# Layer 0's attention product as 64x64 blocks in the four quarters of the array, with a copy of h whose graphs are exchanged

## The chip, the core and the metric

The kernel runs on one core of a Trainium2 chip. Everything is in fp32. The metric is the device time of one execution in microseconds, lower being better. The kernel before takes 3661.84 us, the median of three runs that lie between 3660.82 and 3661.86.

A core has a matrix engine (TensorE, PE in the profile), whose weight loads are shown apart (PEld), and VectorE (DVE), ScalarE (ACT), GpSimd (POOL) and SyncE (SP), which here issues all DMAs. Matmul results land in PSUM, all other data is in SBUF. Both memories have 128 partitions.

## What is computed

The input x holds 128 graphs of 64 nodes with 768 features. Two attention layers follow each other, each with a residual and a layernorm. The change concerns layer 0, cut here to what matters:

```python
h = jnp.einsum('bnd,ade->bane', feat_in, W)              # 12 heads of 64
th = jnp.tanh(h)
attn_src = jnp.einsum('bane,aeo->bano', th, w_src)
attn_dst = jnp.einsum('bane,aeo->bano', th, w_dst)
attn = attn_src + jnp.swapaxes(attn_dst, 2, 3)
attn = jnp.where(attn >= 0, attn, LEAKY_ALPHA * attn)
attn = jnp.where(mask, jnp.float32(-999.0), attn)
attn = jax.nn.softmax(attn, axis=-1)                     # 64 x 64 for each graph and head
feat_out = jnp.einsum('banm,bame->bane', attn, h) + b
feat_out = jax.nn.elu(feat_out)
gate = jax.nn.sigmoid(feat_in @ H_w.T + H_b)
x = layernorm(x + gate * feat_out + (1.0 - gate) * feat_in)
```

The fourth line from the end, the probabilities of a graph times h, is the aggregation that is changed. For one graph and one head it is a product of two 64x64 matrices. Layer 1 is ordinary attention with 6 heads of 128 over the same graphs.

## The kernel before

**Tiles, units, groups.** A tile is 128 tokens on the partitions, that is two graphs of 64 nodes; there are 64 tiles. A unit of layer 0 is half the heads (6 of 12, 384 columns) of one tile, so there are 128 units. A group is two tiles, thus four units. Layer 1 works by groups.

**One unit of layer 0** runs through four functions, two of them a unit later:

- `l0_products(u)` makes h in PSUM (six matmuls of 384 columns at L177), copies it to SBUF on VectorE (L246), takes its tanh, forms the source and destination terms of the attention on GpSimd and VectorE, and makes the gate's product.
- `l0_probs(u)` spreads the destination term by one matmul (L280) and runs the mask and the softmax over `s`, 128 partitions (graph, query) by 6 heads by 64 keys.
- `l0_probs_transposed(u - 1)` turns `s`: three 128x128 transposes, two heads in each (L202). A transposed block has head parity and key on its partitions and graph and query on its columns. Four copies of 64x192 (L209) then put the blocks into `pts[0]`, which is 128x128 for each head and block-diagonal over the two graphs; its other blocks were zeroed once at the start.
- `l0_rest(u - 1)` multiplies: six matmuls of a 128x128 block-diagonal stationary with 64 columns of h (L303), into one PSUM tile `po`. Then VectorE adds the bias (L308), and the elu, the gate, the residual and, after a tile's second half, the layernorm follow.

**Order of the work.** The loop at the end emits, for each unit u, the products of u, the transposes of u-1, some pieces of layer 1, the probabilities of u, the rest of u-1, and more pieces of layer 1. `quota` spreads a group's pieces of layer 1 evenly over four units. A framework then sets the order on each engine when the program is built, by the priority of the code's order and by which instructions it takes to be ready; it also chooses VectorE or ScalarE for every `nc.any.tensor_copy`. Within an engine's queue, SP's among them, that order is fixed. All waits are on semaphores which the framework adds.

**Buffers.** `xp` holds 7 tiles of x; a tile stays from its load to the store of the result, and six pieces of H_w pass through the same buffers at the start. `work` has 2 buffers for most tiles and 3 for h. PSUM is split into 4 banks for products (`psm`) and 4 for everything else (`psa`): transposes, L280, the aggregation's `po`, layer 1's scores (L355) and context (L379).

Layer 1's scores at L355 write 64 columns of the array at a time: one graph to PSUM partitions 0 to 63, the other to 64 to 127. Layer 1 has its own block-diagonal tile, `pts[1]`, filled by `probs_transposed`.

Of the kernel before, what the change touches and what calls it, by code (L numbers as in the profile page):

```python
# [9 lines left out]
F32 = mybir.dt.float32  # L10
# [5 lines left out]
P = 128  # L16
# [7 lines left out]
def kernel(  # L24
# [17 lines left out]
    bf: bass.AP,  # L42
    out: bass.AP,
):
    """Two graph-attention layers, each followed by a residual and a layernorm.

    A tile is 128 tokens on the partitions: two graphs of 64 nodes. A group is G tiles, whose
    q and k share a pass over the weights. All products are in fp32.
    """
    nc = tc.nc  # L50
    NB, S, D = x.shape
    A, _, E = W.shape
# [13 lines left out]
    adj_g = adj.rearrange("(q t g) n m -> q (g n) t m", t=G, g=2)  # L66

    const = ctx.enter_context(tc.tile_pool(name="const", bufs=1))
    xp = ctx.enter_context(tc.tile_pool(name="xp", bufs=7))
    big = ctx.enter_context(tc.tile_pool(name="big", bufs=1))  # L70
    work = ctx.enter_context(tc.tile_pool(name="work", bufs=2))
    small = ctx.enter_context(tc.tile_pool(name="small", bufs=3))
    psm = ctx.enter_context(tc.tile_pool(name="psm", bufs=4, space=bass.MemoryType.PSUM))
    psa = ctx.enter_context(tc.tile_pool(name="psa", bufs=4, space=bass.MemoryType.PSUM))

# [1 line left out]
    ident = const.tile([P, P], F32, name="ident")  # L77
    make_identity(nc, ident)
    eye = const.tile([P, S], F32, name="eye")
# [19 lines left out]
        load_x(t)  # L99
    load_adj(0)  # L100

# [1 line left out]
    def rows(src, name):  # L103
        n = src.shape[0]
        t = const.tile([P, n], F32, name=name)
# [45 lines left out]
    bv_c = columns(bv, "bv_c")  # L151
    bf_bc = rows(bf, "bf_bc")

    # Transposed probabilities of AH heads, block-diagonal over the tile's two graphs: only the
    # diagonal blocks are written after this. One for each layer.
    pts = [const.tile([P, AH, P], F32, name=f"pt{i}") for i in range(2)]
    for pt in pts:
        nc.gpsimd.memset(pt, 0.0)

# [1 line left out]
    def halves(h):  # L161
        return slice(h * HALF, (h + 1) * HALF)

    def transposed(src, dst):
        """dst[:, c, :] = src[:, chunk c].T"""
        for half in range(2):
            ps = psa.tile([P, CH, P], F32, name="pa")
            for c in range(CH):
                k = half * CH + c
                nc.tensor.transpose(ps[:, c, :], src[:, k * P : (k + 1) * P], ident)  # L170
            nc.any.tensor_copy(dst[:, half * CH : (half + 1) * CH, :], ps)  # L171

    def product(lhsT, w, half):
        """One half of the columns of lhsT.T @ w in PSUM."""
        ps = psm.tile([P, HALF], F32, name="pm")
        for c in range(NC):
            nc.tensor.matmul(  # L177
                ps, lhsT[:, c, :], w[:, c, halves(half)], start=(c == 0), stop=(c == NC - 1)
            )
        return ps  # L180

    def softmax(s, n):
        """Over the last of s [P, n, S], in place."""
        mx = small.tile([P, AH], F32, name="mx")
        nc.vector.tensor_reduce(mx[:, :n], s, AX.X, ALU.max)  # L185
        nc.vector.tensor_tensor(
            s, s, mx[:, :n, None].to_broadcast([P, n, S]), ALU.subtract
        )
        nc.scalar.activation(s, s, AF.Exp)
        sm = small.tile([P, AH], F32, name="sm")  # L190
        nc.vector.tensor_reduce(sm[:, :n], s, AX.X, ALU.add)
        rs = small.tile([P, AH], F32, name="rs")
        nc.vector.reciprocal(rs[:, :n], sm[:, :n])  # L193
        nc.gpsimd.tensor_tensor(  # L194
            s, s, rs[:, :n, None].to_broadcast([P, n, S]), ALU.mult
        )

    def probs_transposed(s, pt):
        """s [P, AH, S] over (graph, query) -> [(graph, key), head, (graph, query)]."""
        ps = psa.tile([P, AH // 2, P], F32, name="pa")  # L200
        for j in range(AH // 2):
            nc.tensor.transpose(  # L202
                ps[:, j, :], s[:, 2 * j : 2 * j + 2, :].rearrange("p h m -> p (h m)"), ident
            )
        pt_v = pt.rearrange("p (j h) n -> p j h n", h=2)
        for g in range(2):
            own = slice(g * S, (g + 1) * S)
            for h2 in range(2):
                nc.any.tensor_copy(pt_v[own, :, h2, own], ps[h2 * S : (h2 + 1) * S, :, own])  # L209
# [20 lines left out]
        nc.vector.tensor_scalar(f1, a, 1.0, -L1_NEG, op0=ALU.subtract, op1=ALU.mult)  # L230
        masks[g] = (a, f0, f1)

# [1 line left out]
    xTs, units = {}, {}  # L234

    def l0_products(u):
        t, half = divmod(u, 2)
        hs = halves(half)
        if half == 0:
            xTs[t] = work.tile([P, NC, P], F32, name="xT")  # L240
            transposed(xs[t], xTs[t])
        xT = xTs[t] if half == 0 else xTs.pop(t)

        ph = product(xT, w_sb, half)
        h = work.tile([P, HALF], F32, name="h", bufs=3)
        nc.vector.tensor_copy(h, ph)  # L246
        th = work.tile([P, HALF], F32, name="th")
        nc.scalar.activation(th, ph, AF.Tanh)  # L248
        tmp = work.tile([P, HALF], F32, name="tmp", bufs=3)
        nc.gpsimd.tensor_tensor(tmp, th, ws_bc[:, hs], ALU.mult)  # L250
        sd = small.tile([P, 2, AH], F32, name="sd")
        nc.vector.tensor_reduce(
            sd[:, 0, :], tmp.rearrange("p (a e) -> p a e", a=AH), AX.X, ALU.add
        )
        nc.gpsimd.tensor_tensor(th, th, wd_bc[:, hs], ALU.mult)
        nc.vector.tensor_reduce(
            sd[:, 1, :], th.rearrange("p (a e) -> p a e", a=AH), AX.X, ALU.add
        )
        # dst on the diagonal: what same_graph spreads along the free axis
        dg = work.tile([P, AH, S], F32, name="tmp", bufs=3)  # L260
        nc.gpsimd.tensor_tensor(
            dg,
            eye[:, None, :].to_broadcast([P, AH, S]),
            sd[:, 1, :, None].to_broadcast([P, AH, S]),
            ALU.mult,
        )

        # gate = (1 + tanh(y / 2)) / 2
        pg = product(xT, hw_sb, half)
        gt = work.tile([P, HALF], F32, name="gt")  # L270
        nc.vector.tensor_tensor(gt, pg, hb_bc[:, hs], ALU.add)
        nc.scalar.activation(gt, gt, AF.Tanh, scale=0.5)
        units[u] = [h, gt, sd, dg]

    def l0_probs(u):
        g, i = divmod(u // 2, G)
# [14 lines left out]
        units[u][2:] = [s]  # L291

    def l0_probs_transposed(u):
        probs_transposed(units[u].pop(), pts[0])

    def l0_rest(u):
        t, half = divmod(u, 2)
        hs = halves(half)
        xt = xs[t]
        h, gt = units.pop(u)  # L300
        po = psa.tile([P, AH, E], F32, name="pa")
        for a in range(AH):
            nc.tensor.matmul(  # L303
                po[:, a, :], pts[0][:, a, :], h[:, a * E : (a + 1) * E], start=True, stop=True
            )
        # elu(z) + 1 = max(z, 0) + exp(min(z, 0))
        z = work.tile([P, HALF], F32, name="z")
        nc.vector.tensor_tensor(  # L308
            z.rearrange("p (a e) -> p a e", a=AH),
            po,  # L310
            b_bc[:, None, :].to_broadcast([P, AH, E]),
            ALU.add,
        )
        e = work.tile([P, HALF], F32, name="tmp", bufs=3)
        nc.vector.tensor_scalar_min(e, z, 0.0)  # L315
        nc.scalar.activation(e, e, AF.Exp)  # L316
        nc.vector.scalar_tensor_tensor(z, z, 0.0, e, op0=ALU.max, op1=ALU.add)
        nc.vector.scalar_tensor_tensor(
            z, z, 1.0, xt[:, hs], op0=ALU.subtract, op1=ALU.subtract
        )  # L320
        # the residual's sum, doubled, as the layernorm's epsilon then is fourfold:
        # 2 * (2 * x + gate * (elu - x)) = 4 * x + (1 + tanh(y / 2)) * (elu - x)
        nc.vector.scalar_tensor_tensor(z, gt, 1.0, z, op0=ALU.add, op1=ALU.mult)  # L323
        nc.vector.scalar_tensor_tensor(  # L324
            xt[:, hs], xt[:, hs], 4.0, z, op0=ALU.mult, op1=ALU.add
        )
        if half == 1:
            layernorm(xt, 4.0 * EPS)

# [1 line left out]
    def layer1(g):  # L331
        x1T = big.tile([P, NC, G, P], F32, name="x1T")
        for i in range(G):
# [39 lines left out]
        def context(i):  # L373
            cTs[i] = work.tile([P, HEADS, P], F32, name="cT", bufs=1)
            for half in range(2):
                pc = psa.tile([P, CH, P], F32, name="pa")
                for j in range(CH):
                    hd = half * CH + j
                    nc.tensor.matmul(  # L379
                        pc[:, j, :],  # L380
                        vs[i][:, hd * P : (hd + 1) * P],
                        pts[1][:, hd, :],
                        start=True,
                        stop=True,
                    )
                # a row's probabilities sum to one, so v's bias goes straight to the context
                hds = slice(half * CH, (half + 1) * CH)
                nc.vector.tensor_tensor(  # L388
                    cTs[i][:, hds, :], pc, bv_c[:, hds, None].to_broadcast([P, CH, P]), ALU.add
# [13 lines left out]
        pieces += [(0, probs, (i,)) for i in range(G)]  # L403
        pieces += [(4, values, (0, 0)), (4, values, (0, 1))]
        for i in range(G):
            pieces.append((1, lambda i: probs_transposed(s[:, i], pts[1]), (i,)))
            if i + 1 < G:
                pieces.append((4, values, (i + 1, 0)))
            else:
# [5 lines left out]
        pieces += [(4, result, (G - 1, 0)), (4, result, (G - 1, 1))]  # L415
        return pieces

# [1 line left out]
    assert G == 2  # L419
    UG = 2 * G  # L420
    LAG = 2
# [62 lines left out]
```

## Time and profile before

| | us |
|---|---|
| median of the runs | 3661.84 |
| span of the profiled execution, first to last instruction | 3657.3 |
| TensorE busy | 3605.6 |
| VectorE busy | 1721.5 |
| ScalarE busy | 810.4 |
| GpSimd busy | 852.3 |

The profile is of one execution, and its span lies 4.5 us under the median of the runs. Times in the profile count from its first instruction. L303 is line 303 of the kernel. In a line on a group of instructions stand the line, the engine, the operation, what is written and read, the size and the count; then busy time and the mean duration of one in ns; then the engine's idle time just before them and what ended it. In a line of a timeline stand the start and the time covered by all instructions of that line. Matmuls are pipelined, so their durations overlap: what one costs is the distance from its start to the next. A matmul in fp32 shows as two instructions, each with its own load of weights.

A group of four units takes 112.6 us in the steady part; the first units, without layer 1 beside them, are slower than their matmuls as one chain of small steps has nothing to fill its waits.

### The profile page before, as it was taken

The numbers are of one execution on the slowest core, as the hardware profiler recorded it, in microseconds if no ns is written. First come the engines' busy times: TensorE is split into PE (matmuls) and PEld (weight loads), VectorE is DVE, ScalarE is ACT, GpSimd is POOL, SyncE is SP. The second block draws the span as 40 slices with busy tenths as digits, with TensorE's granted clock in tenths as the row PEclk, the third lists the DMA queues.
The fourth block names the chain that finished last, engine by engine and source line by source line (L and its number), as shares of the span: only waits on it lengthen the run. The fifth ranks groups of instructions, "written<-read, shape, count | busy, mean of one in ns | idle before, by whom it ended". The sixth has DMA issues, their size and how long they took to land.

```text
span 3657.3 us, 40929 instructions
## 1 busy us (share of the span) xinstructions
PE 3605.6 (99%) x16228; PEld 2544.3 (70%) x16228; DVE 1721.5 (47%) x3821; ACT 810.4 (22%) x1925; POOL 852.3 (23%) x904
## 2 busy tenths in 40 slices
PE   6999999999999999999999999999999999999999
PEld 4776677766777666777667776677766677766776
DVE  4545444544444454444544454444445444454442
ACT  2222222222222222222222222222222222222221
POOL 2222212222222222122222222222222222222120
PEclk9999999999999999999999999999999999999999
DMA  6000000000000000000000000000000000000000
GB/s 204 1 18 18 18 10 9 18 18 18 9 10 18 18 18 10 9 18 18 18 18 9 9 18 18 18 9 10 18 18 18 9 10 18 18 18 14 5 5 18
DMA packets 44031, 69.25 MB, mean 19 GB/s; under 512 B 23104, under 2 KB 23104, under 8 KB 43840
## 3 DMA queue, kind: packets, MB, share of 16 engines
q1 hardware_dynamic: 43840, 66.64, 5.3%
q8 instruction: 128, 2.10, 0.2%
q14 instruction: 63, 0.52, 0.0%
HBM read 41.46 MB, written 25.17 MB: 18 GB/s over the span
## 4 chain that ended last, share of the span: by engine, by line
PE 88%; DVE 9%; POOL 1%; ACT 1%; SPq 0%; issue 0%; DMA 0%; POOLq 0%; ACTq 0%
PE pm L177 47%; PE pm L345 28%; PE pa L303 3%; PE pa L280 3%; PE pa L379 2%; PE pa L355 2%; PE pa L202 1%; DVE st L214 1%; POOL s L284 1%; DVE x L396 1%; PE pa L170 1%; DVE z L323 1%; DVE s L287 1%; DVE x L324 1%; DVE mx L185 1%; DVE s L283 1%
## 5 line engine op out<-in xcount | busy, mean ns | idle before, releaser
L345 PE MATMUL pm<-x1T,wq_sb 128*128 128x256 f32 x2304 | 560.3, 384 | 0.3 <-DVE x1T L171 0.3
L177 PE MATMUL pm<-w_sb,xT 128*128 128x384 f32 x1536 | 534.3, 494 | 13.9 <-DVE xT L171 13.4
L345 PE MATMUL pm<-x1T,wk_sb 128*128 128x256 f32 x2304 | 528.6, 379 | 0.0
L177 PE MATMUL pm<-wv_sb,x1T 128*128 128x384 f32 x1536 | 519.8, 488 | 0.0
L177 PE MATMUL pm<-wf_sb,cT 128*128 128x384 f32 x1536 | 517.9, 487 | 0.4 <-DVE cT L388 0.4
L177 PE MATMUL pm<-hw_sb,xT 128*128 128x384 f32 x1536 | 516.3, 486 | 0.0
L345 PEld LDWEIGHTS pm<-x1T,wk_sb 128*128 128x128 f32 x2304 | 437.8, 190 | 59.5
L345 PEld LDWEIGHTS pm<-x1T,wq_sb 128*128 128x128 f32 x2304 | 424.9, 190 | 62.6 <-DVE x1T L171 0.6
L177 PEld LDWEIGHTS pm<-hw_sb,xT 128*128 128x128 f32 x1536 | 291.8, 190 | 203.5
L177 PEld LDWEIGHTS pm<-w_sb,xT 128*128 128x128 f32 x1536 | 284.6, 190 | 199.8 <-DVE xT L171 21.1
L177 PEld LDWEIGHTS pm<-wf_sb,cT 128*128 128x128 f32 x1536 | 286.9, 190 | 187.3 <-DVE cT L388 0.7
L177 PEld LDWEIGHTS pm<-wv_sb,x1T 128*128 128x128 f32 x1536 | 284.3, 190 | 173.4
L358 DVE SCALAR_TENSOR_TENSOR s<-pa,fill 128x128 f32<-128x128 f32 x192 | 54.9, 286 | 661.7 <-PE pa L355 661.7
L250 POOL TENSOR_TENSOR tmp<-th,ws_bc 128x384 f32<-128x384 f32 x128 | 127.6, 997 | 903.7 <-ACT th L248 872.8
L194 POOL TENSOR_TENSOR s<-s,rs 128x384 f32<-128x384 f32 x192 | 177.2, 930 | 666.3 <-DVE rs L193 666.3
L284 POOL TENSOR_TENSOR s<-s,adjf 128x384 f32<-128x384 f32 x128 | 127.7, 998 | 717.1 <-DVE s L283 717.1
L209 ACT COPY pt<-pa 64x192 f32<-64x192 f32 x637 | 199.6, 313 | 428.0 <-PE pa L202 407.3
L303 PEld LDWEIGHTS pa<-h,pt 128*128 128x128 f32 x1536 | 195.4, 194 | 35.3 <-ACT pt L209 1.2
L246 DVE COPY h<-pm 128x384 f32<-128x384 f32 x128 | 71.3, 557 | 285.1 <-PE pm L177 285.1
L248 ACT ACTIVATE th<-pm 128x384 f32<-128x384 f32 x128 | 62.9, 491 | 592.6 <-DVE h L246 592.6
L303 PE MATMUL pa<-h,pt 128*128 128x64 f32 x1536 | 189.1, 273 | 0.1
L316 ACT ACTIVATE tmp<-tmp 128x384 f32<-128x384 f32 x128 | 66.9, 523 | 474.4 <-DVE tmp L315 474.4
(65 smaller groups left out, 3482.8 us busy)
## 6 DMA issues: line engine op xcount, KB each, us to landing
x<-in_x_dram SPq DMA_DIRECT2D x64, 384.0 KB, 2.9
out_dram<-x SPq DMA_DIRECT2D x64, 384.0 KB, 2.3
w_sb<-in_L_gnn_W_dram SPq DMA_DIRECT2D x6, 384.0 KB, 6.3
x<-in_L_gnn_H_w_dram SPq DMA_DIRECT2D x6, 384.0 KB, 7.2
wq_sb<-in_L_gnn_Wq_dram SPq DMA_DIRECT2D x6, 384.0 KB, 6.4
wk_sb<-in_L_gnn_Wk_dram SPq DMA_DIRECT2D x6, 384.0 KB, 7.8
wv_sb<-in_L_gnn_Wv_dram SPq DMA_DIRECT2D x6, 384.0 KB, 7.8
wf_sb<-in_L_gnn_Wf_dram SPq DMA_DIRECT2D x6, 384.0 KB, 7.8
```

The lines of the kernel that those rows point to most:

```text
L177: nc.tensor.matmul(ps, lhsT[:, c, :], w[:, c, halves(half)], start=(c == 0), stop=(c == NC - 1))
L194: nc.gpsimd.tensor_tensor(s, s, rs[:, :n, None].to_broadcast([P, n, S]), ALU.mult)
L209: nc.any.tensor_copy(pt_v[own, :, h2, own], ps[h2 * S : (h2 + 1) * S, :, own])
L246: nc.vector.tensor_copy(h, ph)
L250: nc.gpsimd.tensor_tensor(tmp, th, ws_bc[:, hs], ALU.mult)
L280: nc.tensor.matmul(pd, same_graph, dg, start=True, stop=True)
L284: nc.gpsimd.tensor_tensor(s, s, adjf[:, i, None, :].to_broadcast([P, AH, S]), ALU.mult)
L303: nc.tensor.matmul(po[:, a, :], pts[0][:, a, :], h[:, a * E : (a + 1) * E], start=True, stop=True)
L316: nc.scalar.activation(e, e, AF.Exp)
L345: nc.tensor.matmul(ps, w[:, c, cols], x1T[:, c, :, :], start=(c == 0), stop=(c == NC - 1))
L355: nc.tensor.matmul(pc[own, i, :], qk[0][:, i, own], qk[1][:, i, own], start=True, stop=True)
L379: nc.tensor.matmul(pc[:, j, :], vs[i][:, hd * P : (hd + 1) * P], pts[1][:, hd, :], start=True, stop=True,)
```

## The change

The transposed probabilities are no longer spread into a block-diagonal tile. One copy takes the three transposed blocks as they are, 128x384, into a tile `pt0` of two buffers. Partitions 0 to 63 then hold the keys of even heads, 64 to 127 those of odd heads, and the columns hold both graphs' queries.

The aggregation reads from it 64x64 blocks: head parity `h2` picks the rows, graph `g` the columns. [...]For even heads of graph 0 and odd heads of graph 1 that is h itself; for the other two, h of graph 0 is wanted on the upper partitions or h of graph 1 on the lower. So each unit also keeps `hx`, h with its two graphs exchanged, made by two DMAs from SBUF to SBUF on SP's queue. A unit has 12 matmuls at this place where it had 6. Even and odd heads go to two PSUM tiles, so the bias is added in two steps of 192 columns.

`xp` has 6 buffers instead of 7, which makes room for `hx`. `pts` shrinks to layer 1's tile, `pt1`.

```diff
-    xp = ctx.enter_context(tc.tile_pool(name="xp", bufs=7))
+    xp = ctx.enter_context(tc.tile_pool(name="xp", bufs=6))
...
-    pts = [const.tile([P, AH, P], F32, name=f"pt{i}") for i in range(2)]
-    for pt in pts:
-        nc.gpsimd.memset(pt, 0.0)
+    pt1 = const.tile([P, HEADS, P], F32, name="pt1")
+    nc.gpsimd.memset(pt1, 0.0)
...
         nc.vector.tensor_copy(h, ph)
+        hx = work.tile([P, HALF], F32, name="hx", bufs=2)
+        nc.sync.dma_start(hx[:S, :], h[S:, :])
+        nc.sync.dma_start(hx[S:, :], h[:S, :])
...
-        units[u] = [h, gt, sd, dg]
+        units[u] = [(h, hx), gt, sd, dg]
...
     def l0_probs_transposed(u):
-        probs_transposed(units[u].pop(), pts[0])
+        s = units[u].pop()
+        ps = psa.tile([P, AH // 2, P], F32, name="pa")
+        for j in range(AH // 2):
+            nc.tensor.transpose(
+                ps[:, j, :], s[:, 2 * j : 2 * j + 2, :].rearrange("p h m -> p (h m)"), ident
+            )
+        pt = work.tile([P, AH // 2, P], F32, name="pt0")
+        nc.any.tensor_copy(pt, ps)
+        units[u].append(pt)
...
-        h, gt = units.pop(u)
-        po = psa.tile([P, AH, E], F32, name="pa")
-        for a in range(AH):
-            nc.tensor.matmul(
-                po[:, a, :], pts[0][:, a, :], h[:, a * E : (a + 1) * E], start=True, stop=True
-            )
+        hs_, gt, pt = units.pop(u)
+        pos = [psa.tile([P, AH // 2, E], F32, name="pa") for _ in range(2)]
+        for j in range(AH // 2):
+            for g in range(2):
+                for h2 in range(2):
+                    a = 2 * j + h2
+                    rows_ = slice(h2 * S, (h2 + 1) * S)
+                    own = slice(g * S, (g + 1) * S)
+                    nc.tensor.matmul(
+                        pos[h2][own, j, :],
+                        pt[rows_, j, own],
+                        hs_[g ^ h2][rows_, a * E : (a + 1) * E],
+                        start=True,
+                        stop=True,
+                    )
         z = work.tile([P, HALF], F32, name="z")
-        nc.vector.tensor_tensor(
-            z.rearrange("p (a e) -> p a e", a=AH),
-            po,
-            b_bc[:, None, :].to_broadcast([P, AH, E]),
-            ALU.add,
-        )
+        z_v = z.rearrange("p (j h e) -> p j h e", h=2, e=E)
+        for h2 in range(2):
+            nc.vector.tensor_tensor(
+                z_v[:, :, h2, :],
+                pos[h2],
+                b_bc[:, None, :].to_broadcast([P, AH // 2, E]),
+                ALU.add,
+            )
```

More of the change, by code (lines that the diff above doesn't have):

```diff
@@ L299, in l0_rest @@
         xt = xs[t]
-        h, gt = units.pop(u)
-        po = psa.tile([P, AH, E], F32, name="pa")
-        for a in range(AH):
-            nc.tensor.matmul(
-                po[:, a, :], pts[0][:, a, :], h[:, a * E : (a + 1) * E], start=True, stop=True
-            )
-        z = work.tile([P, HALF], F32, name="z")
-        nc.vector.tensor_tensor(
-            z.rearrange("p (a e) -> p a e", a=AH),
-            po,
-            b_bc[:, None, :].to_broadcast([P, AH, E]),
-            ALU.add,
-        )
+        hs_, gt, pt = units.pop(u)
[13 more added lines that the diff above has]
+                    )
+        z = work.tile([P, HALF], F32, name="z")
+        z_v = z.rearrange("p (j h e) -> p j h e", h=2, e=E)
[5 more added lines that the diff above has]
+                ALU.add,
+            )
         e = work.tile([P, HALF], F32, name="tmp", bufs=3)
@@ L381, in context @@
                         vs[i][:, hd * P : (hd + 1) * P],
-                        pts[1][:, hd, :],
+                        pt1[:, hd, :],
                         start=True,
@@ L405, in layer1 @@
         for i in range(G):
-            pieces.append((1, lambda i: probs_transposed(s[:, i], pts[1]), (i,)))
+            pieces.append((1, lambda i: probs_transposed(s[:, i], pt1), (i,)))
             if i + 1 < G:
```

## The prediction

> **What bounds the kernel now.** I read the busy shares and the shares of the chain first, then the groups by line, then TensorE's timeline through one unit, then the chain of waits in the one stretch where TensorE stops.
>
> ```profile
> PE 3605.6 (99%) x16228; PEld 2544.3 (70%) x16228; DVE 1721.5 (47%) x3821; ACT 810.4 (22%) x1925; POOL 852.3 (23%) x904
> ...
> PE 88%; DVE 9%; POOL 1%; ACT 1%; SPq 0%; issue 0%; DMA 0%; POOLq 0%; ACTq 0%
> ...
> L303 PEld LDWEIGHTS pa<-h,pt 128*128 128x128 f32 x1536 | 195.4, 194 | 35.3 <-ACT pt L209 1.2
> ...
> L303 PE MATMUL pa<-h,pt 128*128 128x64 f32 x1536 | 189.1, 273 | 0.1
> ```
>
> TensorE is the bound: it is idle for 52 us only, 21 of them before its first matmul. So what counts is TensorE's time in L303. The busy times overlap and don't give it; starts do. Each matmul of the code is two of the trace's, so a unit has 12 at L303:
>
> ```profile
> 2012.29 4.03 PE L177 MATMUL pm<-wf_sb,cT 128*128 128x384 f32 x12
> 2016.15 1.45 PE L303 MATMUL pa<-h,pt 128*128 128x64 f32 x12
> 2017.44 4.09 PE L177 MATMUL pm<-wf_sb,cT 128*128 128x384 f32 x12
> 2021.37 2.13 PE L170 MATMUL pa<-ident,x 128*128 128x128 f32 x18
> ...
> 2024.27 4.14 PE L177 MATMUL pm<-w_sb,xT 128*128 128x384 f32 x12 [0.45 <-DVE xT L171]
> ```
>
> Before L303, 12 matmuls of 384 columns take 3.86 us, 0.322 each. L303 takes 1.29 us, and the product after it 3.93, 0.06 more than 3.86, as its weights couldn't be loaded ahead. So a unit's aggregation costs 1.35 us, 0.11 an instruction: 64 columns stream in half of that, and the load of 128 weight columns does not hide behind them.
>
> The nearest thing to the new block is L355, which already writes 64-column halves of the array:
>
> ```profile
> 2045.04 1.03 PE L345 MATMUL pm<-x1T,wq_sb 128*128 128x256 f32 x4
> 2045.99 0.45 PE L355 MATMUL pa<-kT,qT 128*64 128x64 f32 x8
> 2046.38 1.99 PE L345 MATMUL pm<-x1T,wq_sb 128*128 128x256 f32 x8
> 2048.21 0.38 PE L345 MATMUL pm<-x1T,wk_sb 128*128 128x256 f32 x1
> ```
>
> L345 runs at 0.216 an instruction, so its four stream until 2045.90; L355 begins 0.09 later, lasts 0.39, and the eight behind it need 1.83 instead of 1.73. All told 0.58 us for eight. Its single instructions start as four pairs, 6 ns apart in a pair, the pairs 0.100, 0.058 and 0.058 apart: two halves of the array work at once, a round takes about 0.057, and 0.58 - 4 x 0.057 = 0.35 is the price of changing the array's division and back.
>
> The last view is the chain of waits in the same group:
>
> ```profile
> 2011.80 0.66 PE pa L280 x2
> 2012.46 0.02 issue
> 2012.49 0.57 DVE s L282
> ...
> 2018.25 0.43 DVE z L308
> ...
> 2023.76 0.47 DVE xT L171
> 2024.23 0.04 issue
> 2024.27 8.01 PE pm L177 x24
> ```
>
> For 11.7 us VectorE's queue sets the time, and TensorE stands 0.6 us before 2024.27 (30 times, once in four units). In that stretch faster matmuls buy nothing.
>
> [...]
>
> **The change part by part.** Sums are made against the profiled execution: span 3657.3 us, 4.5 under the median of 3661.84, carried over as a constant.
>
> *The matmuls.* 12 a unit become 24, all 64x64, order: row half fastest, then column half. The unknown is how many quarters work in one round. If four: 0.35 + 6 x 0.057 = 0.69 us. If two: 0.35 + 12 x 0.057 = 1.03. If each waits for the one before: 0.35 + 24 x 0.057 = 1.72. I take four: column halves already overlap in L355[...]. Both bounds stay for the range. Gain a unit 1.35 - 0.69 = 0.66 us. It counts in three of four units of each of the 30 steady groups: 90 x 0.66 = 59 us. In the fourth TensorE only waits longer for xT.
>
> *The evacuations.* Four copies at L209 (0.31 on ScalarE, 0.36 on VectorE) become one of 128x384, 0.48 (as the xT copies on ScalarE) or 0.56: about 0.8 us less a unit, on engines with spare time (ScalarE 22%). Nothing waited for them (L303 idles 1.2 us in all for pt), so no gain. L308's one add of 0.55 becomes two of 128x192 from PSUM. L358's 128x128 takes 0.29 and L308's own 128x384 0.55, so 0.35 each, 0.15 more a unit. In three units that is hidden beside TensorE; in the DVE-bound stretch it is on the path: 30 x 0.15 = 4.6 us.
>
> *The exchange.* Two DMAs a unit of 96 KB on SP, 0.33 us of issue each. h was copied at 2006.86 and its L303 is at 2039.38 (the unit after): 32 us against a landing of 2.3 to 2.9. On SP they stand among x loads (longest wait 3.8 us for a store), stores and adj loads, whose long waits (up to 90 us) are for VectorE work that comes in VectorE's own order; behind the exchange wait only stores and x loads. So nothing in the steady part. What it costs if the cover goes: an exchange behind a store that waits 41 us would stop TensorE for some 10 us a group. hx has two buffers: exchange u waits for the matmuls of u-2, which stand before u's product in TensorE's order.
>
> *Two PSUM tiles a unit instead of one* out of four psa buffers: in TensorE's order an L280, L303 and one L355 or L379 tile are beside them, and L282 frees the first about 0.8 us after L280. At L303 then L379 the second half of L379 may wait for it: nothing to 0.3 us in 30 units. I take nothing.
>
> *x buffers, six for seven.* A tile's store stands in unit 4g+9 of the code, and the tile that inherits its buffer (2g+6) is first read in unit 4g+12, over 50 us later, for a load that lands in 2.9. Nothing, in the steady part.
>
> *Start.* SP issues weights until 50.65, and the first exchange (h ready at 32.7) probably comes behind them: issued at 50.7, landing in 2.3 (quiet) to 7.8 (a weight's), so L303 of unit 0, at 49.48 before, starts 4 to 9 us later; take 6. With one x buffer less, the fifth H_w piece waits for the first to be transposed (22.75) as the sixth did: up to 1 us. Sooner pt copies in the first units give about 1 back. Sum 6, between 0 and 10.
>
> Sum: -59 + 4.6 + 6 = -48, to 3614 us.
>
> **Rivals.** *Two quarters at a time.* For it: only column halves are seen overlapping[...]. Gain 90 x 0.32 = 28, less 10.6: 3644 us. *Even.* Rounds near two, a late exchange or groups cut up by 128-row work (in the first units L303 is cut into 2 and 10 by L170 and L177, and each cut would cost another 0.35) eat it: within 0.2%, 7 us, about what a measurement of this kernel can tell from no change. *Slower: quarters that do not overlap.* TensorE would take the 24 short instructions one after another. The price is 0.37 us in each of 90 units, 33 us, plus 10.6: 3706. It decides from 0.042 us an instruction on ((1.35 - 0.35) / 24). For it: the fastest stream over more than 16 instructions in this trace is L303's own, 24 loads and matmuls in 1.29 us, 0.054 each; 48 at that pace would be worse still. Against it: L355's 16 take 0.23.
>
> **How the numbers follow.** Four at a time 0.46, two 0.22, even 0.12, slower 0.20. The likeliest gives 3614, its own range 3597 to 3634 (start 0 to 10, rounds up to 0.07, the stretch of the fourth unit easier or harder by 0.3 us in 30 groups). For 8 in 10 the range goes to 3590 and to 3695, into the slower case. Faster 0.68, same 0.12, slower 0.20.
>
> **What would show it.** Right: starts at the new matmul line in fours some 6 ns apart; the block 0.7 us from the end of the stream before it; the wait for xT at about 1.2 us where it was 0.6; three of four units 0.66 us shorter; no wait for hx after the first units. Wrong: pairs or singles at that line, a wait of TensorE for the exchange, or the block in pieces between 128-row matmuls.

## The result: no difference

The changed kernel takes 3665.55 us, the median of four runs (3661.91 to 3667.56), against 3661.33 for the kernel before, four runs (3659.53 to 3661.86). The ratio is 1.0011, 95% interval 0.9997 to 1.0025, which includes 1. Forecast were 3614 us and a gain of 48. The profiled execution took 3665.66 us and spans 3663.9; against the span before, 3657.3, it is 6.6 longer.

First the busy shares, the shares of the chain and the groups at the new aggregation (L322), from the page of the changed kernel and its groups by line:

```profile
PE 3536.0 (97%) x17764; PEld 2422.5 (66%) x17764; DVE 1743.7 (48%) x3881; ACT 720.7 (20%) x1609; POOL 864.0 (24%) x903
...
PE 86%; DVE 10%; POOL 1%; issue 1%; ACT 1%; SPq 0%; DMA 0%; POOLq 0%; ACTq 0%
...
L322 PE MATMUL pa<-h,pt 64*64 64x64 f32 x1536 | 75.5, 228 | 0.0
L322 PE MATMUL pa<-hx,pt 64*64 64x64 f32 x1536 | 73.3, 228 | 3.4 <-DMA hx<-h 3.4
```

TensorE is busy 70 us less, and yet nothing ends sooner: its idle time went up by 76. VectorE's share of the chain is 10% where it was 9%. Where TensorE stands is seen in its waits (releaser, us in total, times, longest):

```profile
PE pm L176 <- DVE xT L170: 82.8, 31, 4.3
...
PE pa L322 <- DMA hx<-h: 3.4, 1, 3.4
```

The wait for the transposed x (xT) is now 82.8 us, where it was 13.4: 2.6 us in each of the 30 steady groups, where it was 0.45, and 4.3 once at the start. The exchanged copy of h, `hx`, through which the code gives each block rows of h on the block's own partitions, is waited for once, at the start (3.4 us).

The aggregation itself does what was forecast. The timeline of the changed kernel, the end of one product, the block, and the next product:

```profile
2019.44 4.03 PE L176 MATMUL pm<-wf_sb,cT 128*128 128x384 f32 x12
...
2023.41 0.27 PE L322 MATMUL pa<-h,pt 64*64 64x64 f32 x1
...
2023.41 0.27 PE L322 MATMUL pa<-hx,pt 64*64 64x64 f32 x2
...
2023.43 0.30 PE L322 MATMUL pa<-h,pt 64*64 64x64 f32 x2
...
2023.77 0.22 PE L322 MATMUL pa<-h,pt 64*64 64x64 f32 x1
2023.91 4.14 PE L176 MATMUL pm<-wf_sb,cT 128*128 128x384 f32 x12
...
2027.89 2.13 PE L169 MATMUL pa<-ident,x 128*128 128x128 f32 x18
```

The first four instructions start within 0.02 us (single starts lie 7 ns apart), by the code's order one in each quarter, and the last of 24 starts 0.36 after the first. The block and its two changes of the array's division take 0.61 us from the end of the stream before it (2019.44 + 12 x 0.322 = 2023.30) to the next product, and that product needs 3.98 instead of 3.86. That is 0.73 against 1.35 before.

The distance from the start of one unit's product to the next unit's, as median over the steady groups, shows where it goes:

| unit of the group | before | changed | difference |
|---|---|---|---|
| 0 | 27.20 | 26.57 | -0.63 |
| 1 (the distance ends at the product that waits for the next tile's xT) | 22.04 | 23.57 | +1.53 |
| 2 | 32.29 | 31.65 | -0.64 |
| 3 | 31.08 | 30.50 | -0.58 |

Three units win what was forecast, 1.85 us a group or 55.5 us in 30. The unit in which VectorE's queue sets the time loses 1.53, or 46 us. Here is its end in the timeline of the changed kernel (in brackets: idle time before, and what ended it):

```profile
2028.41 0.56 DVE L348 SCALAR_TENSOR_TENSOR z<-gt,z 128x384 f32<-128x384 f32 x1
...
2028.79 3.93 POOL L390 TENSOR_TENSOR x<-x,bf_bc 128x768 f32<-128x768 f32 x2 [2.40 <-PE pa L169]
2029.00 2.06 DVE L349 SCALAR_TENSOR_TENSOR x<-x,z 128x384 f32<-128x384 f32 x1
...
2030.98 0.55 DVE L421 TENSOR_TENSOR x<-pm,x 128x384 f32<-128x384 f32 x1
...
2032.38 0.53 DVE L170 COPY xT<-pa 128x384 f32<-128x384 f32 x1
...
2032.97 3.49 PE L176 MATMUL pm<-w_sb,xT 128*128 128x384 f32 x10 [2.62 <-DVE xT L170]
```

and the same two instructions in the timeline of the kernel before:

```profile
2021.80 0.56 DVE L324 SCALAR_TENSOR_TENSOR x<-x,z 128x384 f32<-128x384 f32 x1
...
2022.27 3.59 POOL L365 TENSOR_TENSOR x<-x,bf_bc 128x768 f32<-128x768 f32 x2 [3.04 <-PE pa L170]
```

L349 (L324 before) is the residual step, x = 4x + z, on VectorE with two operands from SBUF. L390 (L365) is GpSimd's addition of layer 1's last bias to the two tiles of x of the group before. The residual step has the same size and neighbours in both kernels. It takes 0.56 us where it starts before the addition, and 2.06 where the addition is ahead of it by 0.21. In all 30 steady groups of the kernel before the addition starts 0.46 to 0.47 after the residual step, which takes 0.56; in all 30 of the changed kernel it starts 0.20 to 0.21 ahead, and the step takes 2.05 or 2.06. Not every VectorE step suffers: the next one (L421, from 2030.98) has the same size but takes one of its operands from PSUM, runs beside GpSimd's second addition (2030.60 to 2032.72), and takes 0.55.

The addition comes earlier because it overwrites x, which TensorE's transposes for layer 1 (the first 12 of the 18 at L169) must have read: it starts 0.90 us after the first of them in both kernels (2027.89 to 2028.79; before, 2021.37 to 2022.27), behind the six of its own tile. A shorter aggregation brings the transposes forward against VectorE's chain, from 0.43 ahead of the residual step to 1.11, and so the addition from behind that step to ahead of it. The chain of waits of the changed kernel has the delay on the path:

```profile
2025.41 0.50 DVE z L333 x2
...
2029.00 2.06 DVE x L349
2031.06 0.47 DVE x L421
2031.53 0.93 DVE st L213 x2
2032.46 0.47 DVE xT L170
```

Two smaller losses complete the sum. In 7 of the 30 groups the product after this wait is slow; TensorE's timeline has `5.55` us where 4.14 is usual, and the windows around it show why (after the window stand its length, the busy time of PE, PEld, DVE, ACT and POOL with their instructions, then granted clock, DMA share, GB/s):

```profile
2365.99:2369.40 3.41, 1.33 (x13) 1.09 (x10) 3.41 (x5) 1.89 (x5) 3.41 (x2) 1.00 0.02 5
2369.40:2372.81 3.41, 2.88 (x5) 1.65 (x6) 1.43 (x5) 0.00 (x0) 0.84 (x2) 0.50 0.12 50
2372.81:2376.20 3.39, 3.39 (x12) 2.02 (x11) 0.56 (x1) 0.03 (x1) 0.00 (x0) 1.00 0.51 178
```

TensorE is idle for 2.61 us until 2369.93, and the granted clock is halved for 3.41 us from 2369.40 on. Each such group costs 1.45 us, 10 in all. The start, up to the product of unit 10, is later by 7.8, and the end shorter by 1.7. -55.5 + 46 + 10 + 7.8 - 1.7 = +6.6, the difference of the spans.

### The profile page after: what moved, and what is told of

Its sections match the earlier page's. It is cut to its first block, busy times and chain, and to the rows that moved or that the text cites. A ratio compares the mean times of both kernels' runs of the same rounds, so it can differ in the third digit from the quotient of the medians.

```text
span 3663.9 us, 44472 instructions
## 1 busy us (share of the span) xinstructions
PE 3536.0 (97%) x17764; PEld 2422.5 (66%) x17764; DVE 1743.7 (48%) x3881; ACT 720.7 (20%) x1609; POOL 864.0 (24%) x903
## 4 chain that ended last, share of the span: by engine, by line
PE 86%; DVE 10%; POOL 1%; issue 1%; ACT 1%; SPq 0%; DMA 0%; POOLq 0%; ACTq 0%
PE pm L176 48%; PE pm L370 28%; PE pa L283 3%; PE pa L404 2%; PE pa L380 2%; DVE x L349 2%; PE pa L322 1%; DVE st L213 1%; POOL s L287 1%; PE pa L301 1%; DVE x L421 1%; PE pa L169 1%; DVE s L290 1%; PE pa L201 1%; DVE s L285 1%
## 5 line engine op out<-in xcount | busy, mean ns | idle before, releaser
L176 PE MATMUL pm<-w_sb,xT 128*128 128x384 f32 x1536 | 544.6, 502 | 83.0 <-DVE xT L170 82.8
L255 DVE TENSOR_REDUCE sd<-tmp 128x6 f32<-128x384 f32 x128 | 70.8, 553 | 213.8 <-POOL tmp L253 213.8
L188 ACT ACTIVATE s<-s 128x384 f32<-128x384 f32 x192 | 98.7, 523 | 319.6 <-DVE s L185 319.6
L374 ACT ACTIVATE kT<-pm,bk_c 128x256 f32<-128x256 f32 x192 | 91.0, 474 | 293.2 <-PE pm L370 293.2
```

What stands on the lines that cost most here:

```text
L176: nc.tensor.matmul(ps, lhsT[:, c, :], w[:, c, halves(half)], start=(c == 0), stop=(c == NC - 1))
L374: nc.scalar.activation(q, ps, AF.Identity, bias=bias[:, hd : hd + 1])
```

## The experiments

The theory after this reading: the aggregation's gain is whole, and one collision of GpSimd's addition with VectorE's residual step, brought about by TensorE's head start, takes it back. The rivals: the stretch is slower for other reasons (the two bias additions, the order on VectorE), or the exchange and the six x buffers cost something in the steady part. Each ratio is to runs of the kernel before on the same chip, whose medians lie between 3661.2 and 3661.5.

**Without the addition, in both kernels.** These two leave out layer 1's last bias; the order of all other instructions is unchanged.

```diff
-            nc.gpsimd.tensor_tensor(x1, x1, bf_bc, ALU.add)
+            pass
```

> The changed kernel without GpSimd's add of the last bias to layer 0's output (L390), so that the bias is left out; the order on TensorE, VectorE and ScalarE stays the same. Theory, the collision: VectorE's residual step L349 takes 2.06 us once a group because GpSimd's add has just begun[...]. Then L349 stays at 0.56 there, TensorE's gap before the product that waits for xT falls from 2.9 us to about 1.3, the unit with it from 23.6 to 22.1 us, and the time to 3608 us (46 us of the stretch and 10 us of slow matmuls after long gaps gone). Rival, VectorE's stretch is longer by the change's own work there (two adds for one, other copies, their order): nothing of this goes away, 3655 to 3668 us.

> The kernel before without the same add (bias left out). Collision: it has little to remove there, as the longest common case of L324 is 1.07 us in 32 of 128; between 3640 and 3661 us. Rival: 3661 us.

The changed kernel without it takes 3606.37 us, ratio 0.9853 (0.9837 to 0.987). The kernel before without it takes 3659.66, 0.9996 (0.9987 to 1.0004). So GpSimd's work as such costs nothing that can be told from no change; beside the change it costs 59 us (3665.55 less 3606.37). The timeline of the changed kernel without it:

```profile
1993.64 2.13 PE L169 MATMUL pa<-ident,x 128*128 128x128 f32 x18
...
1994.74 0.56 DVE L349 SCALAR_TENSOR_TENSOR x<-x,z 128x384 f32<-128x384 f32 x1
...
1997.21 4.14 PE L176 MATMUL pm<-w_sb,xT 128*128 128x384 f32 x12 [1.11 <-DVE xT L170]
```

TensorE is as far ahead as in the changed kernel (1.10 us), the residual step takes 0.56 in all of these groups, and TensorE waits 1.1 us for xT, close to the 1.2 that the prediction gave for the changed kernel. Unit 1 takes 22.07 us, as before the change, and no product is slowed any more.

**The addition elsewhere in the code.** It was moved from the step of the probabilities to that of the context, with nothing left out; once in the changed kernel, once in the fastest one below.

```diff
         def probs(i):
             softmax(s[:, i], HEADS)
-            x1 = xs[g * G + i]
-            nc.gpsimd.tensor_tensor(x1, x1, bf_bc, ALU.add)
...
         def context(i):
             cTs[i] = work.tile([P, HEADS, P], F32, name="cT", bufs=1)
+            x1 = xs[g * G + i]
+            nc.gpsimd.tensor_tensor(x1, x1, bf_bc, ALU.add)
```

> The changed kernel with all its work, the addition of the last bias to x on GpSimd moved from the step of layer 1's probabilities to the step of its context, some us later in the group. Theory (it is the meeting of this addition with the residual step that costs): the residual step is not above 1.1 us, TensorE's wait for xT falls from 83 to below 40 us, and the time is near the kernel without the addition (3606): 3600 to 3616 us. Rival (the addition costs wherever it stands, by GpSimd's time or by meeting another of VectorE's steps): 3640 to 3668 us.

3668.27 us, 1.0019 (1.001 to 1.0027): missed, and it doesn't test the theory. The timeline of this run (the addition is now L399):

```profile
2023.91 2.13 PE L169 MATMUL pa<-ident,x 128*128 128x128 f32 x18
...
2024.81 3.93 POOL L399 TENSOR_TENSOR x<-x,bf_bc 128x768 f32<-128x768 f32 x2 [2.41 <-PE pa L169]
2025.02 2.06 DVE L349 SCALAR_TENSOR_TENSOR x<-x,z 128x384 f32<-128x384 f32 x1
```

Nothing moved on the chip: GpSimd's instructions come in the same order as in the changed kernel, and the addition still starts 0.90 after the transposes begin, as their reading of x releases it. Its place in the text decided neither.

> The kernel with all copies of transposed x on ScalarE and the first two units' exchanges from ScalarE's queue, with the addition of the last bias moved in the same way. Theory (with those copies on ScalarE TensorE waits for no step of VectorE in the stretch, so the meeting is hidden): within 4 us of that kernel's 3582.5, 3578 to 3586 us. Rival (the meeting still costs something there): 3560 to 3576 us.

3581.72 us, 0.9785 (0.9771 to 0.98). The residual step is at 2.06 in 30 groups here too, so for the same reason this is no more than a repeat of the kernel without the move (3582.51).

**Who copies which half of xT.** The framework chose the engine of each copy. Here it is fixed: ScalarE copies the first half of a tile's xT, VectorE the second, ScalarE all of layer 1's.

```diff
-    def transposed(src, dst):
+    def transposed(src, dst, second):
...
-            nc.any.tensor_copy(dst[:, half * CH : (half + 1) * CH, :], ps)
+            (second if half else nc.scalar.copy)(dst[:, half * CH : (half + 1) * CH, :], ps)
...
-            transposed(xs[t], xTs[t])
+            transposed(xs[t], xTs[t], nc.vector.tensor_copy)
...
-            transposed(xs[g * G + i], x1T[:, :, i, :])
+            transposed(xs[g * G + i], x1T[:, :, i, :], nc.scalar.copy)
```

> The changed kernel with the copies of the transposed x given to fixed engines (first half ScalarE, second VectorE; layer 1's all on ScalarE), as the base for the next run. Both theories: within 10 us of the changed kernel, 3656 to 3675 us.

3618.2 us, 0.9886 (0.9871 to 0.9901): this missed. It was meant as a neutral base for the next run, and it won 47 us. Its timeline:

```profile
2004.21 3.93 POOL L390 TENSOR_TENSOR x<-x,bf_bc 128x768 f32<-128x768 f32 x2 [2.42 <-PE pa L169]
2004.40 2.06 DVE L349 SCALAR_TENSOR_TENSOR x<-x,z 128x384 f32<-128x384 f32 x1
...
2005.32 0.53 ACT L170 COPY xT<-pa 128x384 f32<-128x384 f32 x1
...
2005.90 2.20 PE L176 MATMUL pm<-w_sb,xT 128*128 128x384 f32 x6
...
2008.21 0.55 DVE L170 COPY xT<-pa 128x384 f32<-128x384 f32 x1
...
2008.81 2.20 PE L176 MATMUL pm<-w_sb,xT 128*128 128x384 f32 x6 [0.71 <-DVE xT L170]
```

The collision is there, 2.06 us. But the half that TensorE needs first comes from ScalarE, half the product runs meanwhile, and only 0.71 us of waiting is left. In the changed kernel no matmul of the product starts before VectorE's copy, which suggests that there VectorE has the first half. The reverse was run to see it: the pinned kernel with VectorE on the first half and ScalarE on the second.

```diff
-    def transposed(src, dst, second):
+    def transposed(src, dst, first, second):
...
-            (second if half else nc.scalar.copy)(dst[:, half * CH : (half + 1) * CH, :], ps)
+            (second if half else first)(dst[:, half * CH : (half + 1) * CH, :], ps)
...
-            transposed(xs[t], xTs[t], nc.vector.tensor_copy)
+            transposed(xs[t], xTs[t], nc.vector.tensor_copy, nc.scalar.copy)
...
-            transposed(xs[g * G + i], x1T[:, :, i, :], nc.scalar.copy)
+            transposed(xs[g * G + i], x1T[:, :, i, :], nc.scalar.copy, nc.scalar.copy)
```

> The pinned kernel with the two halves exchanged: the first half of each transposed x is copied by VectorE, the second by ScalarE, as the changed kernel has them in the stretch. Theory (TensorE cannot begin a product before its first half is there, and VectorE delivers that half 1.5 us late behind a residual step of 2.06 us): the gain of pinning (47 us) goes, 3650 to 3672 us, TensorE waits some 80 us for xT and the residual step is again 2.06 us in 30 groups. Rival (pinning helped by giving VectorE less work or another order of it, whichever half it had): 3612 to 3630 us.

3671.03 us, 1.0028 (1.0016 to 1.004). Its units take 26.57, 23.57, 31.65 and 30.50 us, the changed kernel's to the last digit, and its wait for xT is 84.4 us. So the changed kernel pays for the collision because VectorE copies the first half. The framework also gave VectorE one copy of `pt0` a group more here (62 in all, as in the changed kernel) than in the pinned kernel (32), but less work on VectorE is not what helped there: its half came 3.81 us after the start of the residual step (2004.40 to 2008.21), in the changed kernel 3.38 (2029.00 to 2032.38).

**More work for TensorE.** To the pinned kernel, one matmul of 256 columns (0.43 us) was added after the aggregation of one unit in four, which holds TensorE back just ahead of the transposes. Nothing else changes its place in the steady part.

```diff
+        if u % 4 == 0 and u > 0:
+            for _ in range(1):
+                nc.tensor.matmul(
+                    psm.tile([P, HALF], F32, name="pm")[:, :256], pt[:, 0, :], w_sb[:, 0, :256], start=True, stop=True
+                )
```

> The same with one matmul of 256 columns more, whose result nobody reads, behind the aggregation in one unit of four, the one where TensorE waits for xT; the other engines' order is the same. TensorE has 0.43 us more to do in each group. Collision: GpSimd's add now starts after the residual step has begun, so the step takes 0.56 us instead of 2.06 and the time falls by about 50 us against the run before, to some 3615 us. Rival: no change or up to 13 us slower.

3601.04 us, 0.9838 (0.9824 to 0.9853): with 31 matmuls more than the pinned kernel it is 17 us faster. The size was off, as the pinned base had lost most of the wait already; the sign is the point. Its timeline (lines are 5 later, the residual step L354, the addition L395):

```profile
1883.59 2.13 PE L169 MATMUL pa<-ident,x 128*128 128x128 f32 x18
...
1884.25 0.56 DVE L354 SCALAR_TENSOR_TENSOR x<-x,z 128x384 f32<-128x384 f32 x1
1884.49 3.77 POOL L395 TENSOR_TENSOR x<-x,bf_bc 128x768 f32<-128x768 f32 x2 [2.85 <-PE pa L169]
```

TensorE's lead at the transposes is 0.66 us instead of 1.09 (2003.31 to 2004.40), the addition comes 0.24 after the residual step instead of 0.19 ahead, and the step is back at 0.56, in all 30 groups. Unit 1 takes the 0.43 more (21.52 for 21.09), and the wait, which falls in unit 2, goes (31.65 for 32.64): -0.56 x 30 = -17 us. The collision is thus switched off by time alone, with the addition kept.

**All copies of transposed x on ScalarE**, in both kernels, so that TensorE waits for nothing of VectorE's in the stretch:

```diff
-            nc.any.tensor_copy(dst[:, half * CH : (half + 1) * CH, :], ps)
+            nc.scalar.copy(dst[:, half * CH : (half + 1) * CH, :], ps)
```

> The kernel before with all copies of transposed x on ScalarE, so that TensorE no longer waits for VectorE's queue once a group. The wait of 0.6 us in 30 groups goes: 18 us less, 3643 us. Base for the next run.

> The changed kernel with the same copies on ScalarE. Collision: the residual step may still take 2.06 us, but nothing on TensorE waits for it, so the aggregation's gain of about 0.64 us counts in all units: 82 us less than the run before, 7 us of slower start back, so 75 us less, 3568 us; anything from 60 to 80 less supports it. Rival, the gain on TensorE itself is smaller than its block of matmuls shows (other products slower, or more waits elsewhere): under 40 us less.

The kernel before gains 3.4 us: 3658.1, 0.999 (0.9983 to 0.9997). That missed the 18 that were expected: unit 1 falls by 0.31 us only, to 21.73, so half of the gap of 0.6 was not the wait for VectorE (which is gone in this run's trace), and unit 0 rises by 0.22. TensorE's order of transposes and products differs there; whether that is the reason stays open. The changed kernel with the same edit takes 3585.89, 0.9795 (0.9781 to 0.981), 72 us less than its partner, within the 60 to 80 that were to support the theory. Its units take 26.78, 21.09, 31.65 and 30.47 against 27.42, 21.73, 32.29 and 31.06: 0.59 to 0.64 less in all four. Its residual steps still take 2.06 us in 30 groups, and TensorE waits for none of them. This is the change's worth where no queue but TensorE's sets the time.

**The start.** To the last kernel, the first two units' exchanges were put on ScalarE's queue.

```diff
-        nc.sync.dma_start(hx[:S, :], h[S:, :])
-        nc.sync.dma_start(hx[S:, :], h[:S, :])
+        queue = nc.scalar if u < 2 else nc.sync
+        queue.dma_start(hx[:S, :], h[S:, :])
+        queue.dma_start(hx[S:, :], h[:S, :])
```

> The run before with the exchanges of the first two units issued from ScalarE's queue, so that they don't stand behind SP's loads of the weights. The first aggregation then no longer waits for hx: 3 to 6 us less than the run before, if the start's 7 us are that wait; if they come from the x buffers or from weights that land later, under 2 us.

3582.51, 0.9786 (0.9772 to 0.9801), 3.4 us less, though the runs of the two overlap (3581.84 to 3586.14 and 3584.31 to 3590.23). In the changed kernel SP issues the first exchange at 53.43, after its last weights, and TensorE waits 3.39 us for it until 57.08; here it is issued at 35.68, and the wait is gone. Together with its repeat above this is the fastest version found, 2.1% below the kernel before.

**Six x buffers in the kernel before.**

```diff
-    xp = ctx.enter_context(tc.tile_pool(name="xp", bufs=7))
+    xp = ctx.enter_context(tc.tile_pool(name="xp", bufs=6))
```

> The kernel before with six x buffers instead of seven; only SP's order differs. The fifth piece of H_w waits for the first to be transposed: 0 to 3 us more, 3661 to 3664 us, all of it before the first product, nothing in the steady part.

3662.68, 1.0005 (0.9997 to 1.0014): nothing that can be told from no change. In the changed kernel TensorE waits for no load of a tile of x either. That rival falls.

## Why the prediction was wrong

A gain of 48 us was forecast, and none came. The range of 3590 to 3695 holds the time by luck: it reached up to 3695 for the case that the quarters do not overlap, but they do. By the prediction's own steps:

- *The matmuls, 0.66 us a unit by 90 units, 59 us.* Right. Measured 0.63, 0.64 and 0.58 in three units, 55.5 us. That four quarters would work at once was the author's estimate, from the two column halves of L355 in the kernel before. They do, with starts 7 ns apart; rounds take 0.06 us as taken, and the whole came to 0.73 for 0.69, so the price of the two changes of division (0.35) was right within 0.04.
- *"In the fourth TensorE only waits longer for xT."* This is the step that failed. It says that VectorE's chain in the stretch is the same whatever TensorE does before it. TensorE's transposes release GpSimd's addition, and that addition stood 0.47 us behind a VectorE step with which it collides. Bringing TensorE forward by 0.66 moved it ahead. In place of nothing the runs show 46 us of delay in the stretch (1.53 a group, where 0.3 either way was allowed), and 10 of slow products after the longer idle time. Without the addition that step of the prediction holds: wait 1.1 us, unit 1 at 22.07 for 22.04.
- *The choice of numbers that would have shown it.* All were in the timeline before: transposes at 2021.37, residual step at 2021.80, addition at 2022.27. 0.47 of margin is less than 0.66 of gain. The price stood in the same trace, as shown below.
- *The evacuations, +0.15 in the stretch, 4.6 us.* Too large: the two additions at L333 take 0.50 on the chain where the one took 0.43, 0.07 or 2.1 us in 30 groups.
- *The exchange, six x buffers, PSUM tiles in the steady part: nothing.* Right. `hx` is waited for once, at the start, and the run with six buffers shows no cost.
- *The start, 6, between 0 and 10.* 7.8, of which TensorE waited 3.4 for the exchange behind the weights on SP. The rest stays open: without the addition the start is later by 1.7 only, and two profiles with the same order on every engine (the fastest version and its repeat) have starts 3.6 apart.
- *The rival "even"* gave a time near the measured one, for other reasons: no unit's block was cut up, and the rounds were of four. The rival of two quarters and that of quarters that do not overlap both fall with the starts 7 ns apart.

The price could be read in the kernel before, where once a group the same step comes behind another step of GpSimd's:

```profile
1994.40 1.04 POOL L194 TENSOR_TENSOR s<-s,rs 128x384 f32<-128x384 f32 x1 [4.36 <-DVE rs L193]
...
1994.78 1.07 DVE L324 SCALAR_TENSOR_TENSOR x<-x,z 128x384 f32<-128x384 f32 x1
```

L194 begins 0.38 ahead, and the residual step takes 1.07 instead of 0.56, in 31 cases: it ends 0.41 us after L194. An estimate from the kernel before alone: the addition takes 1.82 there and would begin 0.66 - 0.47 = 0.19 ahead, so the step would take 1.82 - 0.19 + 0.41 = 2.04. In the changed kernel it takes 2.06.

On the collision the runs show this much: with the addition 0.21 us ahead, the step takes 2.06; with the addition 0.23 or 0.46 behind, it takes 0.56. In the changed kernel the step ends at 2031.06, 0.41 after GpSimd's first addition (2028.79 to 2030.65), not after the second (until 2032.72). That is less than the 0.56 which the step takes by itself, so some of it ran beside the addition, or the recorded end of the addition is late; which of the two stays open. What the two engines contend for is not shown.

## What to carry to other kernels

When an engine ahead of a waiting stretch gets faster, list what its finished instructions release on the other engines, and how many tenths of a microsecond each of these stands from a step it must not precede: a gain larger than that margin changes the order (here 0.66 us against 0.47). To see what such a meeting costs, look for groups of one instruction with two durations, here 0.56 and 1.07 in the kernel before, and for what ran beside the longer ones. A gain ahead of a stretch that another engine bounds counts only once that engine's queue is out of TensorE's way: giving the first half of the needed tile to ScalarE, which has time to spare (20% busy in the changed kernel), brought 1.1%, giving it all copies of the transposed x about 2%. Moving an instruction in the program can move nothing on the chip, if its place in the queue and its release stay the same: the addition, moved in the text, still began 0.90 us after the transposes.

## What the hardware showed that was not expected

- A VectorE step of 128x384 with two SBUF operands takes 2.06 us instead of 0.56 when GpSimd's addition of 128x768 (1.86 us) began 0.2 us earlier, and 1.07 when a GpSimd step of 1.04 us began 0.38 earlier; both times it ends 0.41 after the GpSimd step. In the run with the added matmul, where the first addition begins 0.23 or 0.24 us after the step, the two additions take 3.77 or 3.78 us together, against 3.59 in the kernel before, where it begins 0.47 after.
- The granted clock was halved for 3.413 us in 7 of the 30 groups, all with an idle time of 2.6 us, and twelve matmuls took 5.55 us instead of 4.14. The halvings begin 450.56 or 563.20 us apart, 132 or 165 times 3.413. In the 3.413 us ahead of each TensorE was busy for 0.32 to 0.39 of the time (1.33 of 3.41 above), its transposes counted; of the other stretches of that length in the steady part, laid end to end from these, the least busy had 0.42. So none of the seven was wholly idle; what sets a halving off is not shown.
- Instructions to the four 64x64 quarters start 7 ns apart, and a round of four takes about 0.06 us, as one of two column halves (L355) did in the kernel before.
